# Four small moves in a four-layer network: a projection product in a tile of the scores, a border tile, a gate and the last layer's tail

## Chip, cores and metric

The kernel runs on one core of a Trainium2 chip. The metric is the device time of one execution in microseconds, median of the runs. "The profile" is one more execution, recorded by the hardware profiler. Engines are named as the profile names them: PE (TensorE; PEld its weight loads), DVE (VectorE), ACT (ScalarE), POOL (GpSimd), SP (the engine that issues most DMAs).

## What is computed

x is (4, 256, 48, 48) in fp32: 4 samples, 256 channels, 2304 positions. It goes through four layers, each with a group norm ahead of it (32 groups) and its result added to x:

```python
x = x + L0(gn(x))   # q, k, v = w_qkv @ x; 8 heads of 64; q, k scaled to length 1;
                    # softmax(10 q k^T) v; w_out @ that + b_out
x = x + L1(gn(x))   # 3x3 max pool, blur to 16x16, sum of four depthwise strips (11x3, 3x11
                    # and two diagonal ones), batch norm, sigmoid; x * that gate, blown up 3x
x = x + L2(gn(x))   # non-local block: softmax(theta phi / 8) g with 64 channels, W @ that,
                    # batch norm over all samples
x = x + L3(gn(x))   # gate a = sigmoid(w2 leaky(w1 mean(x))); depthwise 3x3 of a * x;
                    # instance norm; leaky ReLU
```

## The kernel before

The 128 partitions hold channels, so a sample is two blocks k = 0, 1 of 128 channels by 2304 columns, in SBUF all the time. Columns are worked in 6 chunks of 384 (`SL`).

**Layers 0 and 2: attention in slots.** `attend` walks units (one sample, one pair of heads, one chunk of 384 queries), each in 9 slots of two key blocks. In a slot PE does the scores (L324, 64x64 tiles, into an `sc` tile of two PSUM banks, of which there are 2), ACT their exponentials (L330), DVE adds these up to the softmax sum (L373), and PE weighs the values (L344) with those of the slot before. All other work is a list of jobs hung between a slot's scores and its weighing. A job has a rank, and a slot's jobs run in order of rank; those under 1 come ahead of DVE's sum.

One slot of each unit, the *chunk slot*, carries the projections of the next pair of heads and the output product of a unit already done. Its jobs, by rank: query (L661), values (L695), key (L661), each into a `pj` tile, a PSUM bank; their evictions by ACT (L681 for query and key, L700 for values); and from `out_proj` the two output products. `first` is product 0 (`part(0)`, L759) and DVE's addition of it to x (`onto(0)`, L775); `part(1)` and `onto(1)` are product 1. `total` (L386) adds up the softmax sums in the rest of product 1's bank. `pj` has 2 buffers, dealt in turn. With batch 0 `first` has rank 0, ahead of query; else rank 2.5, between values and key. The last two chunk slots of layer 0 are the case called `soon` after the change and keep their place. While the last sample still attends, layer 2's projections (L1240, L1264) take the projections' place in some chunk slots.

**Layer 1** runs beside the attention, on lanes: generators that are asked for their next piece slot by slot. Most strips are depthwise products of ACT (L990) and sums of DVE (L1013). For the last sample `strips_pe` does them on PE instead: `padded` writes the blurred 16x16 image into a zeroed border tile `pd` (POOL memset L970, DVE L972, ACT L973), DMAs stack shifted copies of it (L1087), and PE multiplies (L1100). `pd` has one buffer, shared by k = 0 and 1. `gated` then forms the gate and applies it to x with six DVE operations, a product and a sum (L1185, L1187) for each third of the rows. For the last sample it is called with `brief=True`, with pieces given out in two slots. Then come the statistics for layer 2's group norm (L1449), its group sums on PE (L233, L247), and layer 2's projections, begun by a bias product (L1204).

**Layer 2** adds the W product (L1315) and its statistics (DVE L1323).

**Layer 3** has a written plan: `at(t, stage, fn)` puts a job into slot t of 48, and a slot's jobs run in order of stage. 8 tiles (sample, block) of 6 slots: PE convolves (L1964), DVE and ACT norm and leak. `GATE_AT` holds, for each sample, the slots of the eight steps of its gate, counted from its first tile; its two PE products are L1895 and L1912. `border(i)` clears tile i's border on POOL (L1794). Per tile, `cv` has `stats` (L2009), `scales` and `shift` (the instance norm's factors), `scale` (ACT L2053), `leak` (DVE L2059), `gain` (the residual, DVE L2064), `store`, in 3 groups of 768 columns. In the tail `keep_up` and `join` do the residual on PE instead (L2079) with an ACT copy (L2091), and `hum` issues filling matmuls (L200). `was` is the last but one tile, `cv` the last.

Of the kernel before, what the change touches and what calls it, by code (L numbers as in the profile page):

```python
# [14 lines left out]
P = 128  # L15
# [63 lines left out]
def usual_path(  # L79
# [16 lines left out]
    def pj_tile():  # L96
        return ps_pj.tile([P, 512], F32, tag="pj", name="pj")
# [650 lines left out]
    def out_proj(b, p, c, pair, o):  # L748

        cols = slice(c * SL, (c + 1) * SL)  # L750

        of = {}

        def part(k):
            of[k] = ps = pj_tile()
            if k:
                of_out["ps"], of_out["t"] = ps, clock["t"]
            n = SL + (c == 0)
            nc.tensor.matmul(  # L759
                ps[:, :n], lhsT=wo[:, p, k * P : (k + 1) * P], rhs=o["o"][:, :n], start=True,  # L760
                stop=True,
            )

        def onto(k):
            ps, n = of[k], SL + (c == 0)
            if c == 0:
                if k == 0:
                    pair["bo"] = small.tile([P, NK], F32, tag="bo", name="bo", bufs=3)
                bo = pair["bo"][:, k : k + 1]
                if p == 0:  # L770
                    nc.vector.tensor_add(bo, ps[:, SL:n], vec[:, V_BOUT, k : k + 1])
                else:
                    nc.vector.tensor_copy(bo, ps[:, SL:n])
            xs = X[b][:, k, cols]
            nc.vector.scalar_tensor_tensor(  # L775
                xs, ps[:, :SL], pair["bo"][:, k : k + 1], xs, ALU.add, ALU.add
            )

        def first():
            part(0)  # L780
            onto(0)

        end = b == B - 1 and p == NPAIR - 1
        return [
            (0.5 if end and c >= NCH - 2 else 2.5 if b else 0, first),
            *[(0.6 if end and c == NCH - 1 else r, fn)
              for r, fn in ((4, lambda: part(1)), (4.2, lambda: onto(1)))],
        ]

# [174 lines left out]
            )  # L964
            yield half

    def padded(k, norm, res):

        pd = lp.tile([P, AS + 2 * PAD, AS + 2 * PAD], F32, tag="pd", name="pd")
        nc.gpsimd.memset(pd, 0.0)  # L970
        rs64 = lp.tile([P, 1], F32, tag="rs64", name="rs64")
        nc.vector.tensor_scalar(rs64, norm["rs"][:, k : k + 1], 1.0 / 64.0, None, ALU.mult)  # L972
        nc.scalar.activation(  # L973
            pd[:, PAD : PAD + AS, PAD : PAD + AS], res["blur"], AF.Identity,
            bias=norm["nb"][:, k : k + 1], scale=rs64,
        )
        return pd
# [60 lines left out]
    def strips_pe(b, norm, res):  # L1038
# [83 lines left out]
        def may_fill(u, n):  # L1122

            k, _, which = ORDER3[u]
            before = [v for v in range(u) if ORDER3[v][2] == which]
            if before and n <= max(m for m, r in enumerate(rounds) if r[0] == before[-1]):
                return False
            if which != "y" and "blurred" not in res[1]:
                return False
            if k not in pd:  # L1130
                if "blurred" not in res[k] or "nb" not in norm:
                    return False
                pd[k] = padded(k, norm, res[k]).rearrange("p r c -> p (r c)")
                res[k]["padded"] = True
                return False
            return True
# [25 lines left out]
    def gated(b, k, norm, res, brief=False):  # L1162

        acc = res["acc"]
        gate = lp.tile([P, AS, AS], F32, tag="gate", name="gate")
        nc.vector.tensor_scalar(
            acc, acc, vec[:, V_M1, k : k + 1], inv1[:, k : k + 1], ALU.subtract, ALU.mult
        )
        if not brief:
            yield 1  # L1170
        nc.scalar.activation(gate, acc, AF.Exp, bias=nb1[:, k : k + 1], scale=-1.0)
        yield 1
        nc.vector.tensor_scalar(gate, gate, 1.0, None, ALU.add)
        nc.vector.reciprocal(gate, gate)
        nc.vector.tensor_scalar(acc, gate, norm["nb"][:, k : k + 1], None, ALU.mult)
        nc.vector.tensor_scalar(
            gate, gate, norm["rs"][:, k : k + 1], 1.0, ALU.mult, ALU.add
        )
        yield 1
        xg = X[b][:, k, :].rearrange("p (r i c j) -> p r i c j", i=3, c=AS, j=3)  # L1180
        up = gate.unsqueeze(3).to_broadcast([P, AS, AS, 3])
        up2 = acc.unsqueeze(3).to_broadcast([P, AS, AS, 3])
        for i in range(4):
            if i < 3:
                nc.vector.tensor_mul(xg[:, :, i], xg[:, :, i], up)  # L1185
            if i > 0:
                nc.vector.tensor_add(xg[:, :, i - 1], xg[:, :, i - 1], up2)  # L1187
            if not brief or i % 2:
                yield 1


# [595 lines left out]
    def border(i):  # L1787
        n, k = TILES[i]
        v = rows_of(i)
        e = edge[:, SEQ[n], k : k + 1]  # L1790
        nc.gpsimd.tensor_copy(
            v[:, 0 : W2 : W2 - 1, :], e.unsqueeze(2).to_broadcast([P, 2, W2])
        )
        nc.gpsimd.tensor_copy(  # L1794
            v[:, 1 : 1 + HW, 0 : W2 : W2 - 1], e.unsqueeze(2).to_broadcast([P, HW, 2])
        )
# [306 lines left out]
    def judge():  # L2103
# [21 lines left out]
        return [(0, MID, lows), (2, SMALL, count), (3, MOMENTS, read), (9, LAST, compare)]  # L2125

    GATE_AT = {
        0: (3, 5, 6, 9, 10, 11, 11, 12), B - 1: (-2, 1, 2, 5, 6, 6, 7, 8),
    }
    for n in range(1, B - 1):  # L2130
        GATE_AT[n] = (-2, 1, 2, 5, 6, 7, 9, 10)
# [24 lines left out]
    def at(t, rank, fn):  # L2156
        events.setdefault(t, []).append((rank, fn))
# [15 lines left out]
    def put_before(t, i):  # L2173

        held = {}
        t += i == 2

        def product(c):
            held[c] = w_product(i, c, w_tile())

        for c in range(L2C):
            at(t - 12 + c, PRODUCT, lambda c=c: product(c))
            at(t - 12 + c, GROW, lambda c=c: grow(i, c, held[c]))
            at(t - 11 + c, SQUARE, lambda c=c: square(i, c))
        at(t - 12, PLACE, lambda: border(i))

    HERE = [
        (-6, 0, (0, 1), "dve"), (-5, 0, (2, 3), "dve"),
# [6 lines left out]
    def put_tile(i, t, cv, final):  # L2195
        for s in range(NSL):
            at(t + s, CONV, lambda s=s: cv.products(s))
        if final:
            for s in range(NSL - 1):
                at(t + s + 1, MOMENTS, lambda s=s: cv.stats(s))  # L2200
            return
        for g in range(NG3):
            at(t + 2 * g + 2, EVICT, lambda g=g: cv.evict(g))
            at(t + 2 * g + 3, SQUARE, lambda g=g: cv.square(g))
        at(t + 2, EVICT, cv.centre)
        soon = t + 2 * NSL == T
        t += 0 if i >= len(convs) - 4 else 3 if cv.k else 5 if t == 0 else 4
        if soon:
            at(t + 9, MOMENTS, lambda: cv.moments(nc.vector))
            at(t + 9, MOMENTS, lambda: cv.scales(nc.vector))  # L2210
            at(t + 10, FRONT, lambda: cv.shift(nc.vector))
            for g in range(NG3):
                at(t + 10, SCALE, lambda g=g: cv.scale(g))
            at(t + 11, LAST, lambda: cv.leak(0))
            return
        if i >= len(convs) - 4:
            t += (7, 5)[cv.k]
            u = t + 3 + cv.k
            at(u, SQUARE, lambda: cv.moments(nc.vector))
            at(u, SQUARE, lambda: cv.scales(nc.vector))  # L2220
            at(u, SQUARE, lambda: cv.shift(nc.vector))
            for g in range(NG3):
                at(t + 5 + g, SCALE, lambda g=g: cv.scale(g))
                u = t + (7, 6)[cv.k] + g
                at(u, LAST, lambda g=g: cv.leak(g))
                at(u, LAST, lambda g=g: cv.gain(g))
                at(u + 1, STORE, lambda g=g: cv.store(g))
            return
        at(t + 8, FRONT, lambda: cv.moments(nc.gpsimd))
        at(t + 8, MOMENTS, cv.scales)  # L2230
        at(t + 8, LAST, cv.shift)
        for g in range(NG3):
            at(t + 9 + g, SCALE, lambda g=g: cv.scale(g))
            u = t + (10 if t == 5 else 11) + g
            at(u, LAST, lambda g=g: cv.leak(g))
            at(u, LAST, lambda g=g: cv.gain(g))
            at(u + 1, STORE, lambda g=g: cv.store(g))
# [25 lines left out]
    cv.aggregate()  # L2263
    cv.scales(nc.vector)
    was = convs[-2]
    cv.shift(nc.vector)
    for g in range(NG3):
        cv.scale(g, cv.ps[g])
    hum(w_all[:, 1, SL:], 12)
    was.keep_up(1, w_all)  # L2270
    was.leak(1)
    was.join(1, w_all)
    was.keep_up(2, cv.ps[0])
    was.leak(2)
    was.join(2, cv.ps[0])
    was.gain(0)
    was.store(0)
    was.store(1)
    for g in range(NG3 - 1):
        cv.leak(g)  # L2280
        cv.gain(g)
# [856 lines left out]
```

## Time and profile before

| | |
|---|---|
| time, median of 3 runs | 3411.63 us (3410.06 to 3414.07) |
| profiled execution, its span | 3412.74 us, 3411.0 us |
| granted TensorE clock | 0.999 |
| PE, weight loads | 3376.7 us (99% of the span), 1678.7 us (49%) |
| DVE, ACT, POOL | 2548.5 (75%), 2289.2 (67%), 616.8 us (18%) |
| L324 scores, layer 0 | 13824 matmuls, 1270.1 us |
| L344 weighing, layer 0 | 13824 matmuls, 1274.9 us |
| L661 query and key | 720 matmuls, 275.4 us, mean 505 ns |
| L695 values | 1080 matmuls, 134.9 us |
| L759 output products | 384 matmuls, 161.8 us, mean 503 ns |

A group of the profile is one line of code on one engine: its busy time, the mean of one instruction, then the engine's idle time just ahead of these instructions with the instruction that ended most of it ("<-"). Busy times of PE add overlapping matmuls once. The times at which two matmuls start are sharper than their lengths: in a plain slot they come in groups of four, of which each costs 0.32 us.

### The profile page before, as it was taken

Reading aid. Unit: us, or ns where it says so; the run is one execution under the profiler, and the core shown is the slowest. Engines: PE = TensorE matmul, PEld = TensorE weight load, DVE = VectorE, ACT = ScalarE, POOL = GpSimd, SP = SyncE. Lnnn points to the kernel's source line nnn. Section 1 sums busy time; section 2 is a strip of 40 time slices with the busy share of each in tenths; the row PEclk is TensorE's granted clock in tenths of the full one; section 3 lists DMA queues with packets and bytes.
Section 4 is the critical chain, followed back from the end, with each engine's and each line's share of the span. In section 5 each row is a group of like instructions: output and inputs, shape, how many; then the busy total and the mean of one; then the engine's idle time right before and its main releaser. Section 6 shows DMA issues by size and latency. Waiting matters only on the chain.

```text
span 3411.0 us, 89437 instructions
## 1 busy us (share of the span) xinstructions
PE 3376.7 (99%) x38038; PEld 1678.7 (49%) x38038; DVE 2548.5 (75%) x3426; ACT 2289.2 (67%) x3679; POOL 616.8 (18%) x617
## 2 busy tenths in 40 slices
PE   9999999999999999999999999999999999999998
PEld 5555455555545444555454445554444444444443
DVE  3455645468788888787888787777887887977777
ACT  5565655565786687556875885558867865555577
POOL 3433333321111010011011000111110110221233
PEclk9999999999999999999999999999999999999999
DMA  2211111111111111131111111111111110231068
GB/s 92 51 23 27 23 27 23 27 22 26 22 33 18 27 23 27 16 83 18 32 18 27 23 27 22 25 23 27 23 22 22 24 26 11 45 71 18 12 150 240
DMA packets 111831, 127.37 MB, mean 37 GB/s; under 512 B 42992, under 2 KB 101824, under 8 KB 110656
## 3 DMA queue, kind: packets, MB, share of 16 engines
q1 hardware_dynamic: 110176, 119.67, 17.5%
q8 instruction: 300, 4.92, 0.6%
q10 hardware_dynamic: 1248, 1.91, 0.2%
q14 instruction: 107, 0.88, 0.1%
HBM read 56.99 MB, written 11.80 MB: 20 GB/s over the span
## 4 chain that ended last, share of the span: by engine, by line
PE 93%; DVE 4%; DMA 1%; issue 0%; POOL 0%; SPq 0%; ACT 0%; DVEq 0%; POOLq 0%; ACTq 0%
PE av L344 36%; PE sc L324 36%; PE pj L661 8%; PE pj L759 4%; PE pj L695 4%; PE cv L1964 2%; DVE acc L373 1%; PE pj L386 1%; PE pj L1240 1%; PE pj L1100 1%; DMA sh<-pad 1%; PE pj L1281 0%; PE pj L1315 0%; SPq L1087 0%; DMA x<-x_out 0%
## 5 line engine op out<-in xcount | busy, mean ns | idle before, releaser
L330 ACT ACTIVATE pt<-sc 128x768 f32<-128x768 f32 x1944 | 1473.4, 810 | 741.4 <-PE sc L324 731.2
L373 DVE TENSOR_TENSOR acc<-acc,pt 128x768 f32<-128x768 f32 x1534 | 1527.0, 995 | 173.7 <-ACT pt L330 71.2
L344 PE MATMUL av<-pt,v 64*64 64x384 f32 x13824 | 1274.9, 484 | 0.0
L324 PE MATMUL sc<-q,k 64*64 64x384 f32 x13824 | 1270.1, 482 | 0.5 <-ACT pt L330 0.5
L324 PEld LDWEIGHTS sc<-q,k 64*64 64x64 f32 x13824 | 525.4, 133 | 589.5 <-issue 556.0
L344 PEld LDWEIGHTS av<-pt,v 64*64 64x64 f32 x13824 | 518.2, 133 | 568.4 <-issue 521.5
L424 POOL TENSOR_TENSOR o<-o,rinv 128x384 f32<-128x384 f32 x95 | 119.7, 1260 | 1707.7 <-DMA rinv<-rinv 1697.6
L775 DVE SCALAR_TENSOR_TENSOR x<-pj,bo,x 128x384 f32<-128x384 f32 x192 | 118.4, 617 | 340.3 <-ACT row L391 184.9
L990 ACT ACTIVATE prod<-pd,wt 128x256 f32<-128x256 f32 x486 | 340.6, 761 | 0.2
L661 PE MATMUL pj<-xs,w 128*128 128x384 f32 (+1 forms) x720 | 275.4, 505 | 0.0
L355 POOL TENSOR_TENSOR half<-pt 128x768 f32<-128x768 f32 x96 | 176.1, 1834 | 378.3 <-ACT pt L330 317.0
L661 PEld LDWEIGHTS pj<-xs,w 128*128 128x128 f32 x720 | 124.1, 189 | 127.9 <-ACT v L700 34.3
L373 DVE TENSOR_TENSOR acc<-acc,half 128x768 f32<-128x768 f32 x96 | 91.7, 955 | 120.5 <-POOL half L355 120.3
L1013 DVE TENSOR_REDUCE prod<-prod 128x256 f32<-128x1280 f32 x114 | 168.7, 1480 | 1.0 <-ACT prod L990 1.0
L759 PE MATMUL pj<-o,wo 128*128 128x384 f32 (+1 forms) x384 | 161.8, 503 | 3.1 <-DVE x L775 2.8
L324 PE MATMUL sc<-qv,kd 64*64 64x384 f32 x1728 | 159.4, 483 | 3.0 <-ACT pt L330 3.0
L344 PE MATMUL av<-pt,qv 64*64 64x384 f32 x1728 | 160.7, 487 | 0.0
L367 DVE TENSOR_TENSOR acc<-pt 128x768 f32<-128x768 f32 x108 | 126.8, 1174 | 31.3 <-ACT pt L330 31.0
L695 PEld LDWEIGHTS pj<-w,xs 128*128 128x128 f32 x1080 | 134.4, 191 | 24.1 <-issue 1.2
L695 PE MATMUL pj<-w,xs 128*128 128x128 f32 x1080 | 134.9, 275 | 0.0
L420 POOL TENSOR_TENSOR o<-raw 128x384 f32<-128x384 f32 x95 | 120.7, 1270 | 45.8 <-ACT raw L416 44.6
L416 ACT COPY raw<-av 128x768 f32<-128x768 f32 x108 | 86.4, 800 | 51.1 <-PE av L344 50.6
(318 smaller groups left out, 2120.1 us busy)
## 6 DMA issues: line engine op xcount, KB each, us to landing
xs<-in_x_dram SPq DMA_DIRECT2D x90, 384.0 KB
sh<-pad SPq DMA_DIRECT2D x122, 162.2 KB
rinv<-rinv SPq DMA_DIRECT2D x208, 94.5 KB
out_dram<-x SPq DMA_DIRECT2D x23, 384.0 KB
w<-in_wqkv_dram SPq DMA_DIRECT2D x32, 192.0 KB
x<-in_x_dram SPq DMA_DIRECT2D x4, 1152.0 KB
x<-in_x_dram SPq DMA_DIRECT2D x9, 384.0 KB
rinv<-ls SPq DMA_DIRECT2D x208, 1.5 KB
```

What stands on the lines that cost most here:

```text
L324: nc.tensor.matmul(ps[c * D : (c + 1) * D, h, :SL], lhsT=u["of"]["k"][r, j0 : j0 + D], rhs=u["of"]["q"][r, u["qc"]], start=True, stop=True,)
L330: nc.scalar.activation(pt, ps[:, :, :SL], AF.Exp, scale=u["scale"])
L344: nc.tensor.matmul(u["av"][h * D : (h + 1) * D, half, :SL], lhsT=value(u, j, h)[r], rhs=pt[r, h, :], start=j == 0, stop=j == JB - 1,)
L355: nc.gpsimd.tensor_add(half, pts[0], pts[1])
L367: nc.vector.tensor_add(u["acc"], ready[0], ready[1])
L373: nc.vector.tensor_add(u["acc"], u["acc"], term)
L420: eng.tensor_add(u["sum"], u["raw"][:, 0, :], u["raw"][:, 1, :])
L661: nc.tensor.matmul(ps[:, :n], lhsT=at["w"][:, k, t, :], rhs=xs[s][:, k, :n], start=k == 0, stop=k == NK - 1,)
L695: nc.tensor.matmul(ps[:, i * P : (i + 1) * P], lhsT=xs[s][:, k, i * P : (i + 1) * P], rhs=at["w"][:, k, 2, :], start=k == 0, stop=k == NK - 1,
L759: nc.tensor.matmul(ps[:, :n], lhsT=wo[:, p, k * P : (k + 1) * P], rhs=o["o"][:, :n], start=True, stop=True,)
L990: nc.scalar.activation(bufs[n % 3][:, :, min(n, 1) + i].rearrange("p (r c) -> p r c", c=AS), pd[:, PAD + dr : PAD + dr + AS, PAD + dc : PA ...
L1013: nc.vector.tensor_reduce(to, bufs[n % 3][:, :, : min(n, 1) + len(taps)], AX.X, ALU.add)
```

## The change

Four edits:

1. `out_proj`: product 0 of a sample b > 0 (except in the last two chunk slots of layer 0) goes into half of an `sc` tile instead of a `pj` tile, and `first` has rank 1.5 instead of 2.5: after query, ahead of values.
2. `strips_pe`: for k = 1 the border tile is taken and cleared one slot before `padded` writes it; before, both were in one slot.
3. `gated`: for k = 1 the last sample's x-operations are given out in four slots (1, 2, 2 and 1 operations) instead of two (3 and 3).
4. Layer 3: the last sample's gate steps come up to two slots earlier; `border(i)` two slots later; the last but one tile's norm factors and scales one slot earlier; its `leak` and `gain` for groups 0 and 1 in slots 46 and 47 with their stores, where `leak(0)` alone stood in slot 47 and the rest in the tail. The tail keeps `leak(2)` and `join(2)` of it; `hum` and the other join are gone, and `keep_up(2)` stands ahead of the last `shift`.

```diff
@@ out_proj
-            of[k] = ps = pj_tile()
+            of[k] = ps = pj_tile() if k or b == 0 or soon else sc_tile()[:, 0, :]
...
+        soon = end and c >= NCH - 2
         return [
-            (0.5 if end and c >= NCH - 2 else 2.5 if b else 0, first),
+            (0.5 if soon else 1.5 if b else 0, first),
@@ padded
-    def padded(k, norm, res):
-
-        pd = lp.tile([P, AS + 2 * PAD, AS + 2 * PAD], F32, tag="pd", name="pd")
-        nc.gpsimd.memset(pd, 0.0)
+    def padded(k, norm, res, pd=None):
+
+        if pd is None:
+            pd = lp.tile([P, AS + 2 * PAD, AS + 2 * PAD], F32, tag="pd", name="pd")
+            nc.gpsimd.memset(pd, 0.0)
@@ strips_pe, may_fill
-                pd[k] = padded(k, norm, res[k]).rearrange("p r c -> p (r c)")
+                if k and "empty" not in res[k]:
+                    res[k]["empty"] = lp.tile(
+                        [P, AS + 2 * PAD, AS + 2 * PAD], F32, tag="pd", name="pd"
+                    )
+                    nc.gpsimd.memset(res[k]["empty"], 0.0)
+                    return False
+                pd[k] = padded(k, norm, res[k], res[k].get("empty"))
+                pd[k] = pd[k].rearrange("p r c -> p (r c)")
@@ gated
-            if not brief or i % 2:
+            if not brief or k or i % 2:
                 yield 1
@@ layer 3
-        0: (3, 5, 6, 9, 10, 11, 11, 12), B - 1: (-2, 1, 2, 5, 6, 6, 7, 8),
+        0: (3, 5, 6, 9, 10, 11, 11, 12), B - 1: (-2, -1, 0, 3, 4, 4, 5, 6),
...
-        at(t - 12, PLACE, lambda: border(i))
+        at(t - 10, PLACE, lambda: border(i))
...
         if soon:
-            at(t + 9, MOMENTS, lambda: cv.moments(nc.vector))
-            at(t + 9, MOMENTS, lambda: cv.scales(nc.vector))
-            at(t + 10, FRONT, lambda: cv.shift(nc.vector))
+            at(t + 8, MOMENTS, lambda: cv.moments(nc.vector))
+            at(t + 8, MOMENTS, lambda: cv.scales(nc.vector))
+            at(t + 9, FRONT, lambda: cv.shift(nc.vector))
             for g in range(NG3):
-                at(t + 10, SCALE, lambda g=g: cv.scale(g))
-            at(t + 11, LAST, lambda: cv.leak(0))
+                at(t + 9, SCALE, lambda g=g: cv.scale(g))
+            for g in range(NG3 - 1):
+                at(t + 10 + g, EVICT, lambda g=g: cv.leak(g))
+                at(t + 10 + g, EVICT, lambda g=g: cv.gain(g))
+                at(t + 11, STORE, lambda g=g: cv.store(g))
...
     was = convs[-2]
+    was.keep_up(2, w_all)
     cv.shift(nc.vector)
     for g in range(NG3):
         cv.scale(g, cv.ps[g])
-    hum(w_all[:, 1, SL:], 12)
-    was.keep_up(1, w_all)
-    was.leak(1)
-    was.join(1, w_all)
-    was.keep_up(2, cv.ps[0])
     was.leak(2)
-    was.join(2, cv.ps[0])
-    was.gain(0)
-    was.store(0)
-    was.store(1)
+    was.join(2, w_all)
     for g in range(NG3 - 1):
         cv.leak(g)
         cv.gain(g)
```

## The prediction

> **What bounds the kernel.** I read the page first, then layer 0's weight loads alone, then one slot of the timeline, then the three places that the other edits touch.
>
> The page's part 1 (engine, busy us, share of the span, instructions) and the ends of the chain:
>
> ```profile
> PE 3376.7 (99%) x38038; PEld 1678.7 (49%) x38038; DVE 2548.5 (75%) x3426; ACT 2289.2 (67%) x3679; POOL 616.8 (18%) x617
> ...
> PE 93%; DVE 4%; DMA 1%; issue 0%; POOL 0%; SPq 0%; ACT 0%; DVEq 0%; POOLq 0%; ACTq 0%
> ```
>
> TensorE sets the end nearly everywhere, at a granted clock of 0.999. So a change pays where it shortens PE's own row, or in the tail, where DVE sets the end. "99% busy" hides how well PE runs: 590 ns instead of 486 ns for one matmul is busy time too. Weight loads show it (layer 0, 900 to 1600 us; last column: what PEld waited for):
>
> ```profile
> L661 PEld LDWEIGHTS pj<-xs,w 128*128 128x128 f32 x184 | 31.2, 189 | 38.3 <-ACT v L700 12.3 <-issue 11.4 <-DVE acc L373 1.2
> L759 PEld LDWEIGHTS pj<-o,wo 128*128 128x128 f32 x92 | 14.9, 191 | 4.8 <-DVE x L775 1.1 <-issue 0.5
> ```
>
> L661 waits for the copy of v, once in each of 23 chunk slots. One such slot:
>
> ```profile
> 1220.58 1.56 PE L661 MATMUL pj<-xs,w 128*128 128x384 f32 x4
> ...
> 1221.98 1.50 PE L695 MATMUL pj<-w,xs 128*128 128x128 f32 x12
> ...
> 1223.31 0.81 PE L759 MATMUL pj<-o,wo 128*128 128x384 f32 x2
> 1223.52 0.48 ACT L700 COPY v<-pj 128x384 f32<-128x384 f32 x1
> ...
> 1224.04 0.94 PEld L661 LDWEIGHTS pj<-xs,w 128*128 128x128 f32 x4 [0.54 <-ACT v L700]
> 1224.05 1.56 PE L661 MATMUL pj<-xs,w 128*128 128x384 f32 x4
> 1224.16 0.62 DVE L775 SCALAR_TENSOR_TENSOR x<-pj,bo,x 128x384 f32<-128x384 f32 x1 [1.89 <-PE pj L759]
> ...
> 1225.44 0.81 PE L759 MATMUL pj<-o,wo 128*128 128x384 f32 x2
> ...
> 1226.18 0.54 PE L386 MATMUL pj<-acc,step 128*32 128x96 f32 x16
> ```
>
> pj has two buffers, dealt in turn: query A, values B, first product A, key B. Key's load needs B, which the copy of v frees at 1224.0. Start to start, key's first two matmuls come 407 and 427 ns after the one before, where warm ones take 322: 85 + 105 = 0.19 us (in the sums below, 732 for the product's run instead of 645, and 1396 for key's instead of 1292).
>
> **What the skill says.** The Trainium skill, "TensorE: Matmul & The Clock Gate", section "Step-by-step: what each phase is for": the queue pulls a weight load ahead of matmuls in flight. The trace agrees: in the same slot query's later loads start 320 ns ahead of their matmuls, key's first 2 ns ahead. The same page, "LDWEIGHTS (loading the stationary operand)", gives columns / 1.2 ns, 107 ns for 128; the 104 ns by which a first matmul is longer (590 against 486) fit that as an exposed load. "Perfetto Trace Analysis", section "Optimization Strategy", reads the same gap repeated on the busy engine as a shortage of buffers; here the gap names one.
>
> **Part 1, the first product in a scores tile.** Of 70 chunk slots with b > 0 that it moves, 64 have layer 0's projection. Read start to start in the trace: 42 plain ones take 1400 (scores) + 1396 (query) + 1336 (values) + 732 (product) + 1396 (key) + 737 + 467 = 7465 ns. Batch 0's slots, where the product is ahead of query already, have key at 1292 and sum to 7275. Afterwards the deal is query A, values B, key A, second product B. Key waits for query's eviction only, which ended 1222.76, over 0.6 us before any place key can take. Can the cold load merely move on?
> - The moved product waits for the exp of the slot's first scores tile, which ends 0.3 to 0.44 us after query begins; its load is due at 0.97.
> - The second product waits for the copy of v. Values end 0.65 us later than now, so the copy ends near 4.07 us after query begins; the load is due at 1.40 + 0.65 + 1.34 + 0.97 = 4.35. Spare 0.28 us.
> - The next slot's second scores tile waits for the DVE sum (L775, 0.62 us). It is due about 7.9 us after query begins, the sum can begin at 2.4. Spare over 4 us, and 2 us with the worst DVE lag of before.
>
> So about 7273 ns: 64 x 0.19 = **12.2 us**. Six slots stand above their form because the second product waited for the first's DVE sum, in the same buffer: 0.11, 0.56, 0.14, 0.17, 0.58, 0.56 = **2.1 us**. In the six slots with layer 2's projection there is no cold load, but two waited likewise (1240 to 1570 and 3045 ns instead of 1291): 0.36 + 1.86 = **2.2 us**. Both sums go, since that buffer is no longer needed; if DVE is late for the next thing too, they come back, 0 to 4.3.
>
> **Part 2, the border tile cleared a slot earlier.** The timeline before:
>
> ```profile
> 3004.69 0.75 POOL L970 MEMSET pd<- 128x784 f32 x1 [5.86 <-DMA stack<-pd]
> 3005.48 0.60 ACT L973 ACTIVATE pd<-blur,gn_nb,rs 128x256 f32<-128x256 f32 x1 [3.86 <-POOL pd L970]
> 3005.99 1.49 ACT L330 ACTIVATE pt<-sc 128x768 f32<-128x768 f32 x2
> 3006.83 0.21 PEld L324 LDWEIGHTS sc<-qv,kd 64*64 64x64 f32 x8 [2.31 <-ACT pt L330]
> ```
>
> POOL's memset waits until the strips' DMAs have read the old buffer; ACT's write stands from 3002.0 for it, with two exps behind, and PE waits for these. From the last product to the next scores PE took 2.13 us, 0.32 is usual. Now the write is queued behind those exps, a slot on, when the memset is done: **1.8 us**. Sixteen strip fills go a slot later on SP, behind two lane DMAs; the product that reads them has slack. Bounds 1.0 to 1.8.
>
> **Part 3, the last sample's second gate spread.** Six x-operations (L1185, L1187, 0.87 us each) go from 3 + 3 to 1, 2, 2, 1 in four slots; statistics (L1449), group norm and layer 2's start follow two slots later. DVE is busy 32.96 of the 34 us from 3088 to 3122, PE 30.05. The largest PE wait there:
>
> ```profile
> PE pj L233 <- DVE bst L1323: 1.5, 1, 1.5
> ```
>
> DVE's sum of work is unchanged, so a spread saves the late bursts alone: this wait with its gap (1.7 to 2.1) and some 0.5 between. Against that, layer 2's bias product (L1204) comes behind a W product (L1315), needs a pj buffer and waits for DVE's L1323: 0.65 to 1.2. Net **+1.3 us**, bounds 0 and 2.5.
>
> **Part 4, layer 3.** `border` is two slots later on POOL, behind no one: nothing. The last gate (stage `GATE_AT`) comes two slots earlier; its second layer (L1912, 0.55 us of PE) falls where PE stood for the shift DMA, 1.3 us at 3377.0, so partly free. The last but one convolution's leaks and gains of groups 0 and 1 move from the tail into slots 46 and 47, and their stores with them. The tail before:
>
> ```profile
> 3392.81 0.57 DVE L2009 BATCH_NORM_STATS2 in_bn<-cv 128x6 f32<-128x384 f32 x1 [1.60 <-PE cv L1964]
> ...
> 3396.16 1.82 DVE L2059 SCALAR_TENSOR_TENSOR x<-x 128x768 f32<-128x768 f32 x2
> ```
>
> Three operations leave the stretch from shift (3396.25) to the last convolution's first leak (3398.91): of 1.74 + 0.93 us only one leak, 0.87, stays: -1.8. But leak 0, gain 0, leak 1 and gain 1, 3.6 us (gain 1 is new on DVE: PE's join did it), enter 16 us of which DVE has 4.1 idle, in two holes that don't fit them all; the last statistics end about 1.1 later. The filling matmuls (`hum`) and one join leave PE, which idles there: nothing. Net **+0.7 us**, bounds -1 and +1.5. The end is the landing of the last halves; earlier stores only thin what goes ahead of them.
>
> **Sum.** 12.2 + 2.1 + 2.2 + 1.8 + 1.3 + 0.7 = 20.3. The profiled execution took 3412.74 with a span of 3411.0, so 3390.7 and 3392.4; against the median of 3411.63 that gives 3391.3, taken as **3391.5 us**.
>
> **Rivals.**
> - *The cold load moves* to the second product (v's copy has only 0.28 us to spare, one 0.75 us ACT operation ahead of it would use it up). It then costs half or all of the 0.19: 6 or 12 us back, 3397.6 to 3403.7. For it: ACT's queue is full of depthwise products; against: they run while the copy waits for PE anyway. Chance 0.12.
> - *DVE takes it back*: nothing of parts 3, 4 and the eight late slots stays, and L1204 and gain 1 cost 1.2 + 1.0. 3411.6 - 12.2 - 1.8 + 2.2 = 3399.8. For it: DVE is full where parts 3 and 4 work. Against: in layer 0 it has 128 us idle in 700. Chance 0.16.
> - *Slower: scores starve.* Now one of only two scores tiles is held until DVE's sum. If that stalls the next slot's second tile, the 14 us gained must be lost over 70 slots, and 7 more: over 0.3 us a slot, so sums over 4.5 us late in every slot. The latest of before was 2 us. From there on about 3419. Chance 0.03.
>
> The forecast keeps 0.69. Range **3387 to 3400**: the bounds of parts 2 to 4 below, the rivals' nearer halves above. A difference of 0.2%, 6.8 us, is about what this kernel's measurement can tell. Faster 0.94, same 0.04, slower 0.02.
>
> **What would show it.** Key's run 1292 instead of 1396 and the product's 645, with no wait of L661 for v; chunk slots at 7273. No ACT L973 in front of exps at 3005. L233's wait gone and one before L1204. The last convolution's first leak about 0.5 us earlier relative to the last convolution matmul. A cold second product, or scores that wait for L775, would make the prediction wrong.

## The result, and the profile after

The changed kernel takes 3398.02 us (median of 6 runs, 3396.99 to 3399.64), the kernel before 3410.96 us (6 runs): a ratio of 0.9962, 95% interval 0.9949 to 0.9974. That is 12.9 us off where 20.1 were forecast. It lies in the range, 6.5 us above the predicted time, and the interval leaves no doubt that the kernel became faster. The profiled execution took 3399.64 us, its span is 3397.9 us, at a granted clock of 0.997.

Two lines of the page after, busy time and the chain by engine:

```profile
PE 3358.5 (99%) x38006; PEld 1684.5 (50%) x38006; DVE 2549.2 (75%) x3427; ACT 2284.2 (67%) x3678; POOL 625.1 (18%) x617
...
PE 96%; DVE 2%; DMA 1%; issue 1%; ACT 0%; SPq 0%; POOL 0%; DVEq 0%
```

PE's busy time fell by 18.2 us, the span by 13.1. The 18.2 cannot be set against the forecast: 3.9 of them are PE work that left the stretch behind the last convolution (8.80 us before, 4.91 after, above all `hum` and a join), where PE sets no pace. Where time was gained and lost is found by reading when the same instruction starts in the two traces:

| the same point in both traces | before | after | lead, us | lead forecast, us |
|---|---|---|---|---|
| last scores of layer 0 | 2860.71 | 2844.41 | 16.3 | 16.5 |
| strip product behind the border tile (L1100, now L1102) | 3052.49 | 3033.53 | 19.0 | 18.3 |
| last scores of layer 2 | 3245.10 | 3226.42 | 18.7 | 19.6 |
| first convolution of layer 3 | 3265.26 | 3246.59 | 18.7 | 19.6 |
| last convolution of layer 3 | 3392.25 | 3374.92 | 17.3 | |
| end of DVE's last addition | 3404.80 | 3391.47 | 13.3 | 20.3 |

Two losses in this table are the clock's. Twice in the trace after, and not at all in that of before, the granted clock fell to half ahead of the tail. In the lines below the first figures are the stretch and its length in us, then come the busy times of PE, PEld, DVE, ACT and POOL with the number of their instructions, and then the granted clock (the last two are of the DMA):

```profile
3098.27:3101.68 3.41, 3.41 (x26) 2.57 (x22) 3.31 (x7) 0.00 (x0) 0.00 (x0) 0.50 0.00 0
3101.68:3105.00 3.32, 3.32 (x46) 2.53 (x38) 3.01 (x7) 1.70 (x3) 0.00 (x0) 1.00 0.04 6
...
3337.20:3340.62 3.42, 3.42 (x26) 0.99 (x24) 3.31 (x7) 3.39 (x9) 0.00 (x0) 0.50 1.00 346
3340.62:3344.00 3.38, 3.38 (x40) 0.88 (x32) 2.39 (x4) 2.45 (x4) 0.51 (x1) 1.00 0.89 229
```

PE works through all of both stretches, with 26 matmuls in each where the stretch behind it has 46 and 40. Half of 3.41 us is 1.7 us. By this estimate the lead without them would be 20.4 us at the last scores of layer 2 and 20.7 at the last convolution. That is above the forecast, though not by the edits alone: 1.0 us of it is one group of 24 strip products (L1100, at 3076.50 us), which took 2.54 us before and 1.55 after, and 1.55 too with edit 1 alone; why is not known.

So edits 1 and 2 gave what they should, edit 3 next to nothing, and edit 4 lost 4.0 us behind the last convolution. The lines for each follow.

**Edit 1.** Weight loads in layer 0 (893 to 1592 us, the same stretch of work; last column: what PEld waited for):

```profile
L661 PEld LDWEIGHTS pj<-xs,w 128*128 128x128 f32 x192 | 32.7, 190 | 27.1 <-issue 10.8 <-DVE acc L373 1.8 <-POOL o L420 1.2
L759 PEld LDWEIGHTS sc<-o,wo 128*128 128x128 f32 x48 | 9.1, 189 | 6.4
L759 PEld LDWEIGHTS pj<-o,wo 128*128 128x128 f32 x48 | 8.4, 190 | 4.0
```

The wait for the copy of v (12.3 us before) is gone and stands in no other row. The same slot of the timeline as before:

```profile
1217.35 1.56 PE L661 MATMUL pj<-xs,w 128*128 128x384 f32 x4
...
1218.74 0.81 PE L759 MATMUL sc<-o,wo 128*128 128x384 f32 x2
...
1219.38 1.50 PE L695 MATMUL pj<-w,xs 128*128 128x128 f32 x12
...
1219.59 0.62 DVE L775 SCALAR_TENSOR_TENSOR x<-sc,bo,x 128x384 f32<-128x384 f32 x1 [0.55 <-PE sc L759]
1220.61 0.95 PEld L661 LDWEIGHTS pj<-xs,w 128*128 128x128 f32 x4
1220.72 1.46 PE L661 MATMUL pj<-xs,w 128*128 128x384 f32 x4
1220.92 0.48 ACT L700 COPY v<-pj 128x384 f32<-128x384 f32 x1 [0.75 <-PE pj L695]
...
1222.02 0.81 PE L759 MATMUL pj<-o,wo 128*128 128x384 f32 x2
...
1222.75 0.54 PE L386 MATMUL pj<-acc,step 128*32 128x96 f32 x16
```

Key's first load (1220.61) now starts 0.11 us ahead of its matmul, with the last of values' matmuls, which themselves start 0.11 us apart. Start to start: 1396 + 643 + 1338 + 1294 + 737 + 467 and the scores' 1400, 7275 ns; the 42 plain slots take 7275 to 7286 ns. The 64 slots together took 487.5 us before and 473.3 after.

**Edit 2.** The timeline at the border tile:

```profile
2987.20 0.75 POOL L1139 MEMSET pd<- 128x784 f32 x1 [5.38 <-DMA stack<-pd]
...
2987.99 0.61 ACT L975 ACTIVATE pd<-blur,gn_nb,rs 128x256 f32<-128x256 f32 x1 [0.65 <-POOL pd L1139]
2988.01 1.47 PE L324 MATMUL sc<-qv,kd 64*64 64x384 f32 x16
```

ACT still waits for the memset, but 0.65 us instead of 3.86, behind the exps and not ahead of them; the scores start on time. All ten traces of this document agree: the five kernels without edit 2 take 1.28 to 2.13 us from the matmul ahead to these scores, and in the five with it no matmul comes as much as 0.7 us behind the one before.

**Edit 3.** PE's waits in the gate's stretch (3064 to 3106 us):

```profile
PE pj L1324 <- DVE bst L1332: 2.3, 1, 2.3
PE pj L386 <- DVE acc L373: 1.5, 1, 1.5
```

The group sums (L233) no longer wait; the W product (L1315 of before) does, for the same `pj` buffers and the same DVE queue.

**Edit 4.** The end of the last gate, and then the last statistics, first before and then after. `hraw` is the copy of the gate's hidden values out of PSUM, `ga` the gate's exp and reciprocal, `x<-cv` ACT's eviction of a convolution.

```profile
3380.70 0.14 DVE L1902 COPY hraw<-cv 64x1 f32<-64x1 f32 x1
3380.88 0.81 ACT L1976 ACTIVATE x<-cv 128x768 f32<-128x768 f32 x1 [0.23 <-DVE hraw L1902]
...
3385.50 0.17 ACT L1919 ACTIVATE ga<-cv 128x2 f32<-128x2 f32 x1 [1.89 <-DVE in_bn L2009]
...
3387.29 0.16 DVE L1924 TENSOR_SCALAR ga<-ga 128x2 f32<-128x2 f32 x1
...
3394.74 0.32 DVE L2013 BATCH_NORM_AGGREGATE in_mv<-in_bn 128x2 f32<-128x36 f32 x1
```

```profile
3361.47 0.14 DVE L1911 COPY hraw<-cv 64x1 f32<-64x1 f32 x1
3361.65 0.81 ACT L1985 ACTIVATE x<-cv 128x768 f32<-128x768 f32 x1 [3.16 <-DVE hraw L1911]
...
3368.85 0.15 ACT L1928 ACTIVATE ga<-cv 128x2 f32<-128x2 f32 x1
...
3369.03 0.17 DVE L1933 TENSOR_SCALAR ga<-ga 128x2 f32<-128x2 f32 x1 [3.39 <-ACT ga L1928]
...
3382.87 0.32 DVE L2022 BATCH_NORM_AGGREGATE in_mv<-in_bn 128x2 f32<-128x36 f32 x1
```

The hidden product now runs two slots earlier, in spare columns of the second of the two banks of the convolution's PSUM tile of that time. It starts at 3356.78 us, but DVE copies its result out only at 3361.47, when the norm factors, a leak and a gain ahead of it in DVE's queue are done, and ACT's eviction of the same tile stands 3.16 us for that copy (0.23 before). The gate's exp is behind that eviction and other work in ACT's queue, and DVE, which has leaks, gains and statistics queued behind the gate, idles 3.39 us for the exp (for which it did not idle before). Behind it DVE is busy almost without a break until the last statistics, which end 7.9 us after the last convolution matmul has started; before it was 2.45.

### The profile page after: what moved, and what is told of

Read it like the earlier page. It is cut to its first block, busy times and chain, and to the rows that moved or that the text cites. A ratio compares the mean times of both kernels' runs of the same rounds, so it can differ in the third digit from the quotient of the medians.

```text
span 3397.9 us, 89368 instructions
## 1 busy us (share of the span) xinstructions
PE 3358.5 (99%) x38006; PEld 1684.5 (50%) x38006; DVE 2549.2 (75%) x3427; ACT 2284.2 (67%) x3678; POOL 625.1 (18%) x617
## 3 DMA queue, kind: packets, MB, share of 16 engines
q8 instruction: 300, 4.92, 0.6%
## 4 chain that ended last, share of the span: by engine, by line
PE 96%; DVE 2%; DMA 1%; issue 1%; ACT 0%; SPq 0%; POOL 0%; DVEq 0%
PE av L344 37%; PE sc L324 36%; PE pj L661 8%; PE pj L695 4%; PE pj L759 3%; PE cv L1973 2%; PE pj L386 1%; PE sc L759 1%; PE pj L1249 1%; PE pj L1102 1%; DMA sh<-pad 1%; DVE acc L373 1%; PE pj L1290 0%; PE pj L1324 0%; PE w L1727 0%
## 5 line engine op out<-in xcount | busy, mean ns | idle before, releaser
L424 POOL TENSOR_TENSOR o<-o,rinv 128x384 f32<-128x384 f32 x95 | 122.6, 1291 | 1695.5 <-DMA rinv<-rinv 1685.2
L775 DVE SCALAR_TENSOR_TENSOR x<-pj,bo,x 128x384 f32<-128x384 f32 x122 | 75.4, 618 | 278.2 <-ACT row L391 207.1
L700 ACT COPY v<-pj 128x384 f32<-128x384 f32 x96 | 45.9, 478 | 92.3 <-PE pj L695 92.3
```

The costliest lines, as they stand in the source:

```text
L424: eng.tensor_mul(o, o, u["rinv"])
```

## The experiments

In the first set, edit 1 alone, edit 4 taken back, one copy moved to another engine, and edit 3 taken back. They ran on one chip beside the kernel before, 3410.42 us.

**Edit 1 alone.** The kernel before with

```diff
-            of[k] = ps = pj_tile()
+            of[k] = ps = pj_tile() if k or b == 0 or soon else sc_tile()[:, 0, :]
...
-            (0.5 if end and c >= NCH - 2 else 2.5 if b else 0, first),
+            (0.5 if soon else 1.5 if b else 0, first),
```

> The kernel before with edit 1 alone (product 0 in half a scores tile, at rank 1.5). If edit 1 is worth what its chunk slots show (64 x 0.19 us of cold weight load and 4.3 us of late sums), 16.5 us off: 3394.5 us, and faster than the whole change. If the gain of edit 1 depends on the other edits, or part of it is given back in layer 2 or 3, 3398 us or more. In the trace: key's run 1294 ns, chunk slots 7275 ns.

3395.4 us (3393.81 to 3398.96), ratio 0.9956, interval 0.9942 to 0.9970. In the trace chunk slots take 7275 ns. So edit 1 carries the whole gain of the change, and by the medians the other three together lose 2.6 us of it.

**Layer 3 as before.** The changed kernel with every line of the last part of the diff undone, among them

```diff
-        0: (3, 5, 6, 9, 10, 11, 11, 12), B - 1: (-2, -1, 0, 3, 4, 4, 5, 6),
+        0: (3, 5, 6, 9, 10, 11, 11, 12), B - 1: (-2, 1, 2, 5, 6, 6, 7, 8),
...
-            for g in range(NG3 - 1):
-                at(t + 10 + g, EVICT, lambda g=g: cv.leak(g))
-                at(t + 10 + g, EVICT, lambda g=g: cv.gain(g))
-                at(t + 11, STORE, lambda g=g: cv.store(g))
+            at(t + 11, LAST, lambda: cv.leak(0))
```

> The changed kernel with edit 4 taken back: all of layer 3's plan and tail as before. Theory one, edit 4 loses 5 to 6 us (the changed trace enters layer 3 with a lead of 18.7 us and ends with 13.1): 3392.5 us. Theory two, the loss is the chance lateness of one reload DMA in this one trace and edit 4 is neutral: 3397 to 3398 us.

3394.11 us (3391.88 to 3395.27), ratio 0.9950, interval 0.9936 to 0.9963. Between the start of the last convolution matmul and the end of DVE's last addition lie 12.55 us, as in the kernel before, against 16.55 in the changed one. Theory one's direction holds: edit 4 costs about 4 us. That is little beside the intervals, but the slowest of these five runs (3395.27) is faster than the fastest of the changed kernel's six (3396.99).

**The hidden copy on ACT.** One line of the changed kernel:

```diff
             def hidden():
                 of["raw"] = small.tile([D, 1], F32, tag="hraw", name="hraw")
-                (nc.vector.tensor_copy if self.n == B - 1 else nc.scalar.copy)(of["raw"], of["ps"])
+                nc.scalar.copy(of["raw"], of["ps"])
```

> The changed kernel, and only the copy of the last sample's hidden values out of PSUM (hraw) is done by ACT instead of DVE. Theory one: ACT's eviction stood 3.2 us for that copy, behind DVE's leaks and gains, the gate's exp came late and DVE then idled 3.4 us for it: with the copy on ACT that idle goes, 3394.5 us. Theory two: DVE's own queue of leaks, gains and statistics is the bound in the tail and the idle is filled elsewhere: 3397 us or more.

3393.88 us (3392.69 to 3394.48), ratio 0.9950, interval 0.9937 to 0.9964. All of edit 4 is in it (the line that differs stood the same in the kernel before), and it is 4.1 us faster than the changed kernel's median; its slowest run, 3394.48, is faster than any of the changed kernel's. The timeline:

```profile
3355.33 0.15 ACT L1911 COPY hraw<-cv 64x1 f32<-64x1 f32 x1
3355.39 0.80 ACT L1985 ACTIVATE x<-cv 128x768 f32<-128x768 f32 x1
...
3363.01 0.15 ACT L1928 ACTIVATE ga<-cv 128x2 f32<-128x2 f32 x1
3363.19 0.17 DVE L1933 TENSOR_SCALAR ga<-ga 128x2 f32<-128x2 f32 x1 [0.67 <-ACT ga L1928]
```

ACT reads the hidden values in its own order, the eviction has no wait, the exp comes 5.8 us earlier (5.4 when counted from the first convolution) and DVE idles 0.67 us for it instead of 3.39. The tail takes 12.63 us. That this one wait is the loss behind the last convolution is therefore shown and not only argued. The clock does not set the two tails apart: the last join, which starts at 3385.30 us in the changed kernel and at 3380.36 here, runs at half clock in the one (from 3381.58 us on) and for the most part in the other (from 3380.90).

**Edit 3 taken back.** The changed kernel with

```diff
-            if not brief or k or i % 2:
+            if not brief or i % 2:
```

> The changed kernel with edit 3 taken back (x-operations of the last gate 3 + 3 in two slots). If the spread is worth nothing because DVE's sum of work is the same and the wait only moves from the group sums to the W product: within 0.7 us of 3398. If the spread saves what the prediction gave it: 3399.3 us. If it costs: 3397 us or less.

3397.66 us (3397.20 to 3399.62): no difference that the times can show. The waits of PE in the same stretch:

```profile
PE pj L233 <- DVE bst L1332: 1.5, 1, 1.5
PE pj L386 <- DVE acc L373: 1.1, 1, 1.1
PE sc L324 <- ACT pt L330: 1.0, 3, 0.4
```

What PE loses there beyond the usual 0.32 us from start to start sums to 4.55 us here, to 4.92 in the changed kernel (1.65 ahead of L386, 2.44 ahead of L1324, 0.83 ahead of layer 2's bias product L1213) and to 4.92 in the kernel before. The traces of all ten kernels say the same of the whole stretch. Between two scores matmuls that every kernel has (3081.0 and 3162.1 us before), and with 1.7 us taken off for a stretch of half clock where one falls in between, the four with the spread take 80.7 us and the six without it 80.7 to 81.2. So the spread is worth 0 to 0.4 us.

Since edit 4 is in this kernel, its trace has the wait of edit 4 again:

```profile
ACT x L1985 <- DVE hraw L1911: 3.4, 1, 3.4
DVE ga L1933 <- ACT ga L1928: 3.4, 1, 3.4
```

Its tail takes 16.66 us. So the tail tells the kernels apart: 16.55 and 16.66 us with the wait, 12.55 and 12.63 without it.

In the second set, the parts of edit 1, a test of its spare, and one variant of edit 4; the kernel before took 3410.63 us beside them.

**The scores tile at the old rank.** Against edit 1 alone:

```diff
-            (0.5 if soon else 1.5 if b else 0, first),
+            (0.5 if soon else 2.5 if b else 0, first),
```

> Edit 1 alone, with the scores tile but at the old rank 2.5 (product 0 between values and key). If the buffer is what pays, key takes the buffer that query's eviction freed long before and the rank is worth nothing: as edit 1 alone, 3395.4 us, chunk slots 7275 ns. If the rank is needed, because the tile is held 1.3 us longer or product 0 in front of key cools key's load: 3399 us or more.

3395.33 us (3393.07 to 3397.26), ratio 0.9955, interval 0.9938 to 0.9971, chunk slots 7275 ns in the order query, values, product 0, key. The buffer alone gives all of edit 1; the rank gives nothing on top that can be measured.

**The new rank with the old buffer.** Against edit 1 alone:

```diff
-            of[k] = ps = pj_tile() if k or b == 0 or soon else sc_tile()[:, 0, :]
+            of[k] = ps = pj_tile()
```

> Edit 1 alone, with rank 1.5 but the old pj buffer. Values then take the buffer of query, whose eviction ends 2.18 us after query begins; values are due at 2.04 and their load at 1.72. The wait moves from key to values: some 0.28 us lost in place of 0.19, less the late sums that go: 3408 to 3413 us. If the order alone pays: 3395.4 us.

3439.0 us (3436.54 to 3443.7), ratio 1.0081, interval 1.0064 to 1.0098: slower by 28 us, where a change between -3 and +2 us was expected. The plain slot is as I costed it, 7570 ns, but many slots take more, up to 9.4 us, and the 64 slots sum to 515.3 us against 487.5 before. One of them:

```profile
1378.84 0.58 ACT L681 ACTIVATE q<-pj,bias 128x384 f32<-128x384 f32 x1 [0.59 <-PE pj L661]
1379.47 1.41 PEld L695 LDWEIGHTS pj<-w,xs 128*128 128x128 f32 x12 [0.64 <-ACT q L681]
...
1381.14 0.61 DVE L775 SCALAR_TENSOR_TENSOR x<-pj,bo,x 128x384 f32<-128x384 f32 x1
1381.81 0.94 PEld L661 LDWEIGHTS pj<-xs,w 128*128 128x128 f32 x4 [0.92 <-DVE x L775]
```

Values wait for query's eviction, as expected. What I left out: key now takes product 0's buffer, and DVE's sum of product 0 is late (it starts at 1381.14, 1.7 us after product 0 ended), behind two of layer 1's gate operations in DVE's queue. PE's waits of key for L775 alone sum to 14.2 us in 16 slots. In the scores tile the same lateness of DVE hides, since that tile is due only in the next slot.

**Group 1 joined on PE.** Against the kernel with the hidden copy on ACT:

```diff
-                at(t + 10 + g, EVICT, lambda g=g: cv.gain(g))
-                at(t + 11, STORE, lambda g=g: cv.store(g))
+            at(t + 10, EVICT, lambda: cv.gain(0))
+            at(t + 11, STORE, lambda: cv.store(0))
...
-    was.keep_up(2, w_all)
+    was.keep_up(1, w_all)
...
+    was.join(1, w_all)
+    was.store(1)
+    was.keep_up(2, cv.ps[0])
     was.leak(2)
-    was.join(2, w_all)
+    was.join(2, cv.ps[0])
```

> The changed kernel with the hidden copy on ACT, and group 1 of the last but one tile joined on PE in the tail instead of gained by DVE in slot 47. If DVE's queue ahead of the last statistics is what bounds the tail now, 0.93 us less on DVE: 3393.0 us. If something else bounds it (the landing of the last stores, the scale of the last tile on ACT): 3393.9 us, or more as a store comes later.

3394.85 us (3393.17 to 3395.32). The trace's tail is shorter by 1.06 us (11.57 against 12.63), about the 0.93 us that left DVE, but the time is not. This trace was 1.4 us behind that of the hidden copy on ACT at layer 3's start, which a stretch of half clock of 3.41 us from 3099.13 us on can account for, and its last stores land 0.5 us later behind DVE's end. The differences are within what the runs scatter, so it stays open whether this is worth anything.

**The sum of product 0 held late.** Against edit 1 alone (`late` is b > 0 and not `soon`; product 1's sum, rank 4.2, then makes the bias tile):

```diff
         def first():
             part(0)
-            onto(0)
+            if not late:
+                onto(0)
...
+            *([(4.25, lambda: onto(0))] if late else []),
```

> Edit 1 alone, with DVE's sum of product 0 put behind that of product 1, so that the scores tile is held about 4 us longer. By the prediction's spare (next scores tile due 7.9 us after query begins, the sum then ending near 7.2): no stall, 3395.4 us, chunk slots 7275 ns. If scores starve already: each of 70 slots loses, 0.3 us each would be 3416 us.

3397.17 us (3395.66 to 3398.34), ratio 0.9960, interval 0.9946 to 0.9974. Chunk slots are 7275 ns, none above its form, so scores do not starve even with the tile held until behind product 1's sum. The median is 1.8 us above edit 1 alone, and the intervals overlap. In the traces 0.8 us are lost ahead of layer 0's end, where no wait in the chunk slots answers to it, and 1.0 in the one group of strip products that took 2.54 us in the kernel before (2.55 here, 1.55 with edit 1 alone). Whether the late sum costs anything stays open.

## Why the prediction was right or wrong

The time lies in the range, but in the part of it that was kept for the rivals, and for a reason that no rival named: that the range held was in part luck. The four parts fared differently.

**Edit 1: right, by its own steps.** 64 slots by 0.19 us and the late sums of six slots were 14.3 us forecast and 14.1 measured (487.47 to 473.33 us). The two late slots with layer 2's projection gave 2.2 (the 1570 and 3045 ns of L1240 are 1291 and 1292). The loads at values and at the second product were warm and the next slot's scores were on time, so each spare was enough. The runs add that it is the buffer, not the place: this was not asked in the prediction, which reasoned with both together. One reading in it is not shown: that the 104 ns are a load's own length. The trace gives these loads 190 ns in the mean, not 107. The 0.19 us does not rest on this, since it was read from start to start.

**Edit 2: right.** 1.8 us were forecast, and the lead grew by 1.9 across it in the changed trace. The size is the wait of one execution: in the five traces without the edit it was 1.0 to 1.8 us beyond the usual 0.32. The edit was not run alone.

**Edit 3: wrong in the step "so a spread saves the late bursts alone: this wait with its gap".** DVE's backlog at the end of the stretch is the sum of its work, and the spread doesn't change it. The wait at L233 was how the backlog showed and not an extra cost; with the spread it shows at the W product, 2.44 us, and at the bias product, 0.83 (0.65 to 1.2 was forecast). Net 0 to 0.4 us by the traces, of 1.3.

**Edit 4: wrong in the step on the gate, "its second layer (L1912, 0.55 us of PE) falls where PE stood for the shift DMA", which costs the move by PE's time only.** Of a step that is moved every instruction counts. The copy of the hidden values moved too, to a place in DVE's queue behind leaks and gains, and it holds the PSUM tile that ACT has to evict. That gave the chain DVE copy, ACT eviction, ACT exp, DVE gate: 3.39 us of idle where the prediction had +0.7. The Trainium skill, "PSUM — Partial Sum Buffer", section "PSUM bank collisions raise a hardware error", says that accesses of two engines to one bank in the same 32 partitions have to be kept apart, reads against reads included, and that the compiler's scheduler puts a dependency between them. The trace agrees: ACT waits 3.16 us for DVE's read of other columns in that bank. The rest of the step was right in direction. With the wait gone, the last statistics end 1.55 us later against the last convolution than before (1.1 forecast), and from there to the last tile's first leak it takes 1.47 less (1.8 forecast), so behind the last convolution edit 4 without its wait is worth nothing, not 0.7: the loss was 0.45 us larger and the gain 0.33 smaller than forecast.

The other 1.3 us that layer 3 lost lie between the first and the last convolution, 126.99 us before and 128.33 after. The new plan is not needed to explain them: the stretch of half clock from 3337.20 us on costs 1.7 us there, and the trace of before has none. With layer 3 as before, edit 1 alone has such a stretch and takes 128.05 us, and the buffer alone has none and takes 126.98. With the new plan, the hidden copy on ACT has one and takes 127.70, and the kernel without the spread has none and takes 126.07. With 1.7 us taken off for each stretch, nine of the ten traces take 126.0 to 127.0 us; the tenth, the new rank with the old buffer, has a stretch of twice the length, part of which PE waits through, and takes 129.86. PE waited ahead of the stretch too, 3.3 us for DVE's `pad` (L1791), which waits for the reload of x from DRAM; the same wait was 2.5 us with edit 1 alone, so it is not edit 4's either. When the clock falls stays open. In the gate's stretch, PE's wait at the W product has half clock close behind it in two of the four traces with the spread, and the wait at L233 in two of the six without it.

**The rivals.** "DVE takes it back" had the size, 3399.8 against 3398.0, but by operations that add up on a full engine; it was an idle DVE, and one line of code removes most of it. The cold load did not move, and scores did not starve, not even with the tile held about 4 us longer.

## What to carry to other kernels

Where two engines read parts of one PSUM bank, ask in whose queue the smaller read stands. Here a copy of 64 values held the eviction of the tile for 3.16 us, because it stood in the other engine's queue; on the engine that evicts the tile it held nothing. When a step is moved, cost every instruction in it by the queue it enters, not by the engine that it was moved to relieve. A buffer whose release is due only a slot later hides an evictor's lateness that a two-buffer rotation in the middle of a burst shows at once: the same new order cost nothing with the far buffer, and 28 us without it. And before a difference between two traces is put down to a change, compare the granted clock stretch by stretch: its mean over the span, 0.997 against 0.999, hid where 3.4 us went.

## What the runs showed that I had not expected

The order alone costs 28 us in 64 slots though the plain slot is only 0.1 us longer. DVE's sum of product 0 came over 1 us late in 19 slots, up to 2.5; in the kernel before the late sums cost 2.1 us in six slots. Edit 4's move of a 64-element copy of 0.14 us cost 4 us. And eight of the ten traces have one or two stretches at half the granted clock ahead of the last convolution, of 3.41 us each but for one of 6.83, though every span's mean clock is 0.997 or more.
